# Where the first scores of layer one stand, and which weight sum GpSimd takes next

## The chip, the cores and the metric

The kernel runs on one core of a Trainium2 chip. The metric is the device time of one execution in microseconds (us); three runs of the kernel before took 2652.22, 2652.43 and 2653.41 us, median 2652.43. Lines such as L733 are lines of the kernel before. The engines are TensorE (PE, with its weight loads as PEld), VectorE (DVE), ScalarE (ACT), GpSimd (POOL) and SyncE (SP), which issues most transfers.

## The reference, cut to what matters

The inputs are `x` of 128 graphs × 64 nodes × 768 features in float32, an adjacency matrix for each graph, and for each of two layers three 768 × 768 weight matrices (left, right, linear), a bias and the scale and offset of a LayerNorm.

```python
h = jnp.maximum(_layernorm(x), 0.0)
for l in range(2):
    m_left, m_right = h @ W_left[l].T, h @ W_right[l].T
    u_left, u_right = h @ m_left^T / temper, h @ m_right^T / temper   # by graph, 64 x 64
    u = u_left * triu(adj, 1) + u_left * diag(adj) + u_right * triu(adj, 1)^T
    d = exp(u) * adj
    attention = d / (sum(d, axis=2) + 1e-10)
    h = relu(layer_norm(attention @ (h @ W_lin[l].T + b_lin[l]), ln_a[l], ln_b[l]))
out = x + h
```

The "scores" of this document are `u_left` and `u_right`; the tensors `m` are `m_left` and `m_right`.

## The kernel before

A part is 256 tokens (four graphs), kept with features on the partitions; there are 32 parts. Each layer has a first pass (scores and softmax, whose attention goes to DRAM) and a second pass (linear layer, attention product and LayerNorm). The change lies in the first pass of layer one (`l == 0` in the code), which is `pass_one`.

**Plain block and products.** The first pass computes `m_left` and `m_right`. For the first two parts it does so plainly: twelve chains of three 256 × 256 weight blocks (18 raw blocks, in `W[0, "raw"]`), each chain ending in a PSUM bank (C, D, X, Y in turn) that ACT copies into `m0` (first part) or `m1` (second part) at L889. The later parts go three at a time ("supers") by a fast scheme: 40 products (`PRODUCTS`) of a sum of weight blocks and a sum of token blocks; each product is four matmuls at L702, and its bank is read into several pieces of `m` with signs (`READS`; ACT at L910, DVE at L914 and L245). A super of three parts has 40 products; the third part of a super goes to `m2`. In layer one super 1 comes directly behind the plain block.

**Weight sums.** The fast scheme needs about a hundred sums of weight blocks (`W_OPS`). In layer one they are made while PE works on the plain block, and left in the 51 SBUF buffers `g`. `turn_of(slot)` runs twice in each product and hands out work by a model of time, `now = slot * 0.86`: as long as DVE's modelled clock is not ahead of `now`, `Weights.some` issues one more sum on DVE (0.62 us on its clock); if POOL's clock is not ahead, one on POOL (1.35 us). `some` walks the list of open sums in order and takes the first whose operands exist in the program's order; POOL may take only sums without a multiplier, among the first 40 open ones. POOL then goes on to the token sums (`Tokens.step`). Where a sum is the last use of an operand, it overwrites that operand's buffer (`emit`); other buffers come from `free`, which token sums use too.

**Staging.** During the plain block DVE does not read both operands of a sum from SBUF: `weights.stage` is a ring of PSUM banks (Z, V and the bank pair of the scores, sc), ACT first copies one operand into the next bank of the ring (L517), and DVE adds from there (L245, L522). The ring is set at L888 and cleared behind the plain block. 66 sums are staged. ACT's queue holds these copies, the copies into `m` (L889) and LayerNorm work of the next tokens (L412), in the order in which the code issues them; every engine runs its own queue in order.

**Scores and softmax.** `scores(k)` (L733) multiplies the tokens of super k by `m0`, `m1`, `m2` in small matmuls (32 × 95 columns) into sc. It loops over token halves and, inside, over six feature chunks. Each pair of chunks comes from one copy of L889, so a matmul waits only for the copies that its chunk needs. It is issued behind the fourth product of the next super (`i == SCORED`, SCORED is 3), and the banks of the first four products are read only then, since those reads overwrite `m`. `softmax(k)` is a chain of eight steps, put on slots three apart, starting ten slots behind the start of the next super: POOL masks (L745), DVE multiplies sc (L755), ACT takes Exp, DVE normalises, and eight transfers on SP store the attention.

Of the kernel before, what the change touches and what calls it, by code (L numbers as in the profile page):

```python
# [17 lines left out]
def kernel(  # L18
# [12 lines left out]
    nc = tc.nc  # L31
# [35 lines left out]
    def put(slot, *fs):  # L67
        plan.setdefault(slot, []).extend(fs)

    def put_all(slot, fs, step=1):  # L70
        for f in fs:
            if f is not None:
                put(slot, f)
            slot += step
        return slot
# [5 lines left out]
    def run(slot):  # L81
        if slot in plan:
            for f in plan.pop(slot):
                f()
        elif idle:
            f = idle.popleft()
            if f is not None:
                f()
        if background:
            background[0]()  # L90
# [84 lines left out]
    SCORED = 3  # L175
# [145 lines left out]
    KEEP = {}  # L321
# [155 lines left out]

    class Weights:
        def __init__(self, ops, plain, stay, extra=()):
            self.at, self.left, self.stay = {}, list(ops), stay  # L480
            self.uses = {}
            for _, a, _, b, _ in W_OPS:
                for v in (a, b):
                    self.uses[v] = self.uses.get(v, 0) + 1
            for v in range(18):
                self.uses[v] = self.uses.get(v, 0) + plain
            for f in FORMS:
                self.uses[f] = self.uses.get(f, 0) + 1
            self.stage = []
            self.mine = {id(t) for t in extra}  # L490
            self.extra = deque(extra)
# [36 lines left out]
            self.left.remove(op)  # L528
            return True

        def some(self, eng, reach=10):
            for op in self.left[:reach]:
                if op[1] in self.at and op[3] in self.at and (eng is nc.vector or op[2] == 1):
                    if eng is nc.vector and op[2] == 1 and any(o[2] != 1 and o[1] in self.at and o[3] in self.at
                                                               for o in self.left[:reach // 2]):
                        continue
                    return self.emit(eng, op)
            return False

        def need(self, v):  # L540
# [114 lines left out]
    def pass_one(l, start, final):  # L655
        with tc.tile_pool(name=f"one{l}", bufs=2, reuse_waits="tile") as sp, \
# [58 lines left out]
            def into(o, thirds=False):  # L715
                v, k, i = o // 6, o // 3 % 2, o % 3
                if thirds:
                    r, n = THIRDS[v]
                    return both[:, i * K2:(i + 1) * K2, :, k, r + n:r + WIDE]
                return M[v][:, i * K2:(i + 1) * K2, :, k, :]  # L720

            def scores(k):
                nq = 2 * len(SUPER[k])
                p = KEEP["scores"].rearrange("p a (q m) -> p (a q) m", m=P)
                for q in range(nq):
                    ht, m = HT[1, l, SUPER[k][q // 2]], M[q // 2]
                    for c in range(C):
                        for h in range(PAIR):
                            b = q % 2 * PAIR + h
                            mb = both[:, c, q // 2 * PB + b] if l and k == 0 else m[:, c, b]  # L730
                            mb = mb.rearrange("p k j -> p (k j)")
                            for e in (0, 32):
                                nc.tensor.matmul(p[h * S + e:h * S + e + 32, q, e:e + 95],  # L733
                                                 ht[:, c, b * S + e:b * S + e + 32], mb[:, e:e + 95],
                                                 start=(c == 0), stop=(c == C - 1))
# [45 lines left out]
            def softmax(k):  # L781
                CHAIN[k] = chain(k)
                return [lambda: next(CHAIN[k], None)] * 8

            mid = None
            if l == 0:
# [18 lines left out]
                def mid():  # L805
                    for f in turns[1:]:
                        f()
                    load_rows(0, 1, sp)
                    load_rows(0, 2, other)
                    for t in range(2):  # L810
                        nc.sync.dma_start(KEPT[0][t], HT[1, 0, t])
                    load_adj(0)
                    cols.extend([column("a_col", ln_a[0]), column("b_col", ln_b[0])])
# [8 lines left out]
            def bank_of(n):  # L822
                n %= BANKS
                return KEEP["CD"][n] if n < 2 else KEEP["XYZV"[n - 2]]

            weights, tokens = Weights(() if l else W_OPS, 2, True), TOKENS[l]
# [3 lines left out]
            clock = {"pool": 0.0, "vector": 0.0}  # L830

            def turn_of(slot):
                now = slot * 0.86 if l == 0 or slot >= 80 else slot * 0.6 + 20.8
                clock["vector"] = max(clock["vector"], now - 1.0) + sum(getattr(f, "vector", 0.0) for f in plan.get(slot, ()))
                run(slot)
                if fetch and slot >= start["weights"] and slot % 3 and free:
                    fetch.popleft()()
                if weights.left and slot >= start["weights"]:
                    while clock["vector"] <= now and weights.some(nc.vector):
                        clock["vector"] += 0.62  # L840
                    if clock["pool"] <= now and start["pool"] <= slot < start["tokens"]:
                        if weights.some(nc.gpsimd, 40):
                            clock["pool"] = max(clock["pool"], now) + 1.35
                if clock["pool"] <= now + 1.5 and tokens.step(slot):
                    clock["pool"] = max(clock["pool"], now) + 1.35
# [32 lines left out]
            slot = 0  # L878
            for n, (w, t) in enumerate(order):
                bank = bank_of(n % CHAINS)  # L880
                for j in range(3):
                    tok = HT[1, l, t][:, j * K2:(j + 1) * K2, :]
                    product(bank, weights.at[3 * w + j], [tok], j == 0, slot)
                    weights.used(3 * w + j)
                    if j == 2:
                        if n == 0 and mid:
                            mid()
                            weights.stage = [KEEP["Z"], KEEP["V"], KEEP["scores"][:, 0]]  # L888
                        nc.scalar.copy(into(6 * t + w), out_of(bank))  # L889
                    turn_of(slot + 1)  # L890
                    slot += 2
            weights.stage = []

            last = len(SUPER) - 1
            for k in range(FIRST_OF[l], len(SUPER)):
                assert slot == begins(k, l)
                if k:
                    put_all(slot + 2 * SCORED + 4, softmax(k - 1), 3)
                    put(slot + 2 * SCORED + 42, lambda k=k: load_adj(k, nc.scalar))
                if k == last:  # L900
                    final(slot, tokens)
                seen, waiting = set(), []

                def reads(i):
                    for o, c in READS[i]:
                        bank = out_of(bank_of(CHAINS * (k - 1) + i % CHAINS), k == 0, o)
                        to = into(o, k == 0)
                        if o not in seen:
                            seen.add(o)
                            nc.scalar.activation(to, bank, AF.Copy, scale=float(c))  # L910
                        elif abs(c) == 1:
                            added(nc.vector, to, "+" if c > 0 else "-", to, bank)
                        else:
                            nc.vector.scalar_tensor_tensor(to, bank, float(c), to, op0=ALU.mult, op1=ALU.add)  # L914

                for i, (f, t) in enumerate(PRODUCTS):
                    while l and f not in weights.at:
                        fetch.popleft()()
                    w, tok = weights.need(f), tokens.need(k, t)
                    product(bank_of(CHAINS * (k - 1) + i % CHAINS), w, tok, i < CHAINS, slot, TH if k else 2 * CUT)  # L920
                    tokens.used(k, t)
                    if k == last:
                        weights.used(f)
                    waiting.append(i)
                    if i == SCORED and k:
                        scores(k - 1)
                    if i >= SCORED or k == 0:
                        for n in waiting:
                            reads(n)
                        waiting = []  # L930
                    turn_of(slot + 1)
                    slot += 2
# [432 lines left out]
```

## Time and profile before

| what | value |
|---|---|
| runs | 2652.22, 2652.43, 2653.41 us; median 2652.43 |
| profiled execution, whole time | 2648.42 us |
| its span | 2646.6 us |
| mean granted clock of TensorE | 0.995 |
| busy, share of the span | PE 98%, PEld 84%, DVE 67%, POOL 67%, ACT 35% |
| transfers | 331.84 MB, mean 125 GB/s |

The span is the time from the first to the last instruction in the profile; the whole time has 1.8 us more around it. Shares are means over passes with different limits, so what an edit is worth is read in the stretch where it acts. A row of the time line has its start, its length, the engine, the line and operation, the tile written and the tiles read, the number of instructions merged and, in brackets, idle time ahead of it and what ended that. PE's records count double where one float32 matmul takes two instructions: a product of four matmuls is 8 records, the plain block's chain 24, the scores of two parts 192.

### The profile page before, as it was taken

To read this page: it belongs to the slowest core of one execution; us is meant where nothing else is said; L and a number is where in the kernel's file an instruction comes from. 1 tells how busy PE (TensorE), PEld (TensorE's weight loads), DVE (VectorE), ACT (ScalarE), POOL (GpSimd) and SP (SyncE) were. 2 spreads that over 40 slices of the span, in tenths; PEclk is the share of its full clock that TensorE was granted. 3 is DMA by queue.
4 is the path that set the end of the run, shared out by engine and by line. 5 is a ranking of instruction groups with operands and counts; after the bars stand their busy time and mean duration, and the time that the engine had idled before them with its cause. 6 is when DMAs were issued, how large, how long until landed. Compare 5 with 4: busy or idle time off the path is not lost. (4 is left out here: it accounts for less than half of the span.)

```text
span 2646.6 us, 47202 instructions
## 1 busy us (share of the span) xinstructions
PE 2591.6 (98%) x18122; PEld 2217.1 (84%) x18122; DVE 1780.6 (67%) x2888; ACT 935.4 (35%) x1969; POOL 1763.1 (67%) x1392
## 2 busy tenths in 40 slices
PE   9899999999999999999999999999999989999998
PEld 8788888888888888888798888888888878887886
DVE  7878787777768445554456667677666676666667
ACT  5522223223113244454542222122222335555453
POOL 4766676666668657676276666667666657878786
PEclk9999999999999999999999999999999999999999
DMA  7443534343421354445794424253532215555655
GB/s 220 113 111 86 124 93 110 93 119 79 98 60 56 123 156 149 159 139 182 219 282 101 121 68 108 71 129 93 136 98 70 67 49 157 157 167 166 177 161 146
DMA packets 258465, 331.84 MB, mean 125 GB/s; under 512 B 56002, under 2 KB 190402, under 8 KB 258242
## 3 DMA queue, kind: packets, MB, share of 16 engines
q1 hardware_dynamic: 241442, 320.56, 44.3%
q10 hardware_dynamic: 16800, 8.26, 1.2%
q8 instruction: 145, 2.38, 0.4%
q14 instruction: 78, 0.64, 0.1%
HBM read 213.39 MB, written 115.34 MB: 124 GB/s over the span
## 5 line engine op out<-in xcount | busy, mean ns | idle before, releaser
L245 POOL TENSOR_TENSOR g<-ht 128x512 f32<-128x512 f32 (+1 forms) x620 | 785.9, 1279 | 420.8 <-PE Z L702 71.6
L245 POOL TENSOR_TENSOR g<-g,g 128x512 f32<-128x512 f32 (+1 forms) x310 | 397.9, 1291 | 136.7 <-PE C L702 22.0
L245 POOL TENSOR_TENSOR g<-ht,g 128x512 f32<-128x512 f32 (+1 forms) x272 | 346.1, 1282 | 164.8 <-PE Z L702 42.8
L702 PE MATMUL X<-g,g 128*128 128x256 f32 (+1 forms) x1080 | 252.9, 377 | 6.0 <-DVE m L914 6.0
L1006 PE MATMUL Z<-g,g 128*128 128x256 f32 x1024 | 244.1, 380 | 3.5 <-ACT hl L300 3.2
L702 PE MATMUL C<-g,g 128*128 128x256 f32 x1008 | 239.7, 381 | 4.9 <-POOL g L245 2.2
L702 PEld LDWEIGHTS X<-g,g 128*128 128x128 f32 x1080 | 203.0, 191 | 34.8 <-DVE m L914 6.8
L702 PE MATMUL Y<-g,g 128*128 128x256 f32 (+1 forms) x968 | 225.7, 376 | 3.8 <-POOL g L245 3.8
L1006 PEld LDWEIGHTS Z<-g,g 128*128 128x128 f32 x1024 | 191.6, 190 | 35.8 <-issue 4.1
L379 ACT ACTIVATE ht<-ht,b_col,a_col 128x256 f32<-128x256 f32 x384 | 196.1, 591 | 69.0 <-DMA ht<-h 53.8
L702 PEld LDWEIGHTS C<-g,g 128*128 128x128 f32 x1008 | 190.5, 190 | 32.9 <-POOL g L245 3.5
L702 PE MATMUL Z<-g,g 128*128 128x256 f32 (+1 forms) x936 | 217.0, 375 | 0.0
L702 PE MATMUL D<-g,g 128*128 128x256 f32 x880 | 209.8, 381 | 1.8 <-POOL g L245 1.8
L702 PEld LDWEIGHTS Y<-g,g 128*128 128x128 f32 x968 | 182.0, 190 | 27.8 <-POOL g L245 4.2
L702 PE MATMUL V<-g,g 128*128 128x256 f32 (+1 forms) x840 | 194.6, 375 | 3.1 <-POOL g L245 1.6
L702 PEld LDWEIGHTS Z<-g,g 128*128 128x128 f32 x936 | 174.5, 190 | 23.1
L702 PEld LDWEIGHTS D<-g,g 128*128 128x128 f32 x880 | 168.1, 191 | 25.7 <-POOL g L245 2.5
L1006 PE MATMUL X<-g,g 128*128 128x256 f32 x768 | 182.7, 379 | 0.0
L702 PEld LDWEIGHTS V<-g,g 128*128 128x128 f32 x840 | 157.6, 191 | 23.3 <-POOL g L245 1.7
L1206 POOL TENSOR_TENSOR z<-z,b 128x768 f32<-128x768 f32 x62 | 112.7, 1829 | 81.7 <-DVE z L1203 77.2
L245 DVE TENSOR_TENSOR m<-m,Y 128x512 f32<-128x512 f32 (+2 forms) x196 | 126.5, 667 | 58.4 <-ACT m L910 35.7
L245 DVE TENSOR_TENSOR m<-m,D 128x512 f32<-128x512 f32 x180 | 118.2, 677 | 70.0 <-ACT m L910 51.3
(222 smaller groups left out, 4612.0 us busy)
## 6 DMA issues: line engine op xcount, KB each, us to landing
ht<-h SPq DMA_DIRECT2D x126, 768.0 KB, 6.3
h<-xb SPq DMA_DIRECT2D x124, 384.0 KB, 6.6
z<-z SPq DMA_DIRECT2D x128, 192.0 KB, 3.1
x<-z SPq DMA_DIRECT2D x128, 192.0 KB, 5.4
xr<-in_x_dram SPq DMA_DIRECT2D x120, 192.0 KB, 3.8
out_dram<-xr SPq DMA_DIRECT2D x120, 192.0 KB, 2.7
x<-in_x_dram SPq DMA_DIRECT2D x112, 192.0 KB, 5.4
g<-form SPq DMA_DIRECT2D x40, 256.0 KB, 5.6
```

The source lines that it names most:

```text
L245: (eng.tensor_add if sign == "+" else eng.tensor_sub)(o, a, b)
L379: nc.scalar.activation(ht, ht, AF.Relu, bias=cols[1][:, c:c + 1], scale=cols[0][:, c:c + 1])
L702: nc.tensor.matmul(o, w[:, c, g * P:(g + 1) * P], t, start=(new and g == c == at == 0), stop=(c == K2 - 1), skip_group_check=True)
L1006: nc.tensor.matmul(p[:, n], b[t][:, c, r * P:(r + 1) * P], w[s][:, c, :], start=(i in FIRST and i not in PRELOAD and n == c == 0), stop=(c ...
L1206: nc.gpsimd.tensor_add(zs[k], zs[k], rows["b"])
```

## The change

Three things are edited.

1. In layer one, `scores(0)` is issued directly behind the plain block instead of behind super 1's fourth product. The banks of super 1's first four products are then read one by one as each product is issued, and the softmax steps of the plain block start two slots behind the start of super 1 instead of ten.
2. From the ninth chain of the plain block on (`n == 8`) the staging ring is Z and V alone, since sc is to receive the scores.
3. `Weights.some` notes for each sum a modelled time at which it is made: `now + 6.0` on DVE, `now + 1.35` on POOL. For POOL the candidates are sorted by the later of their operands' times, all that lie before `now` counting alike, and the first is taken.

```diff
             self.at, self.left, self.stay = {}, list(ops), stay
+            self.made = {}
...
-        def some(self, eng, reach=10):
-            for op in self.left[:reach]:
+        def some(self, eng, reach=10, now=None):
+            ops = self.left[:reach]
+            if eng is nc.gpsimd:
+                ops = [op for op in ops if op[1] in self.at and op[3] in self.at and op[2] == 1]
+                ops.sort(key=lambda op: max(now, self.made.get(op[1], 0), self.made.get(op[3], 0)))
+            for op in ops:
...
-                    return self.emit(eng, op)
+                    if self.emit(eng, op):
+                        self.made[op[0]] = now + (6.0 if eng is nc.vector else 1.35)
+                        return True
+                    return False
...
                 bank = bank_of(n % CHAINS)
+                if n == 8:
+                    weights.stage = [KEEP["Z"], KEEP["V"]]
...
             weights.stage = []
 
+            if not l:
+                scores(0)
             last = len(SUPER) - 1
...
                 if k:
-                    put_all(slot + 2 * SCORED + 4, softmax(k - 1), 3)
+                    put_all(slot + (2 * SCORED + 4 if l or k > 1 else 2), softmax(k - 1), 3)
...
-                    if i == SCORED and k:
+                    if i == SCORED and l + k > 1:
                         scores(k - 1)
-                    if i >= SCORED or k == 0:
+                    if i >= SCORED or l + k < 2:
                         for n in waiting:
                             reads(n)
```

More of the change, by code (lines that the diff above doesn't have):

```diff
@@ L479, in __init__ @@
         def __init__(self, ops, plain, stay, extra=()):
-            self.at, self.left, self.stay = {}, list(ops), stay
+            self.at, self.left, self.stay, self.made = {}, list(ops), stay, {}
             self.uses = {}
@@ L838, in turn_of @@
                 if weights.left and slot >= start["weights"]:
-                    while clock["vector"] <= now and weights.some(nc.vector):
+                    while clock["vector"] <= now and weights.some(nc.vector, now=now):
                         clock["vector"] += 0.62
                     if clock["pool"] <= now and start["pool"] <= slot < start["tokens"]:
-                        if weights.some(nc.gpsimd, 40):
+                        if weights.some(nc.gpsimd, 40, now):
                             clock["pool"] = max(clock["pool"], now) + 1.35
```

## The prediction

> **What bounds the kernel now.** I read the page's totals first, then TensorE's waits, then the stretch in which its idle time lies, engine by engine.
>
> ```profile
> span 2646.6 us, 47202 instructions
> PE 2591.6 (98%) x18122; PEld 2217.1 (84%) x18122; DVE 1780.6 (67%) x2888; ACT 935.4 (35%) x1969; POOL 1763.1 (67%) x1392
> ```
>
> TensorE (PE) is busy for 98% of the span: all others work beside it, and only what makes it wait, or slows its clock, is on the path. Busy time in four stretches (columns: length, PE busy, granted clock, DMA share, GB/s):
>
> ```profile
> 0.00:74.89 74.89, 71.97 (x346) 1.00 0.80 215
> 74.89:99.49 24.60, 15.78 (x225) 0.79 0.50 127
> 99.49:200.00 100.51, 98.05 (x712) 1.00 0.39 100
> 200.00:2646.00 2446.00, 2405.85 (x16842) 1.00 0.45 124
> ```
>
> The edits act in layer one's first pass, around the end of the plain block. There, between 74.89 and 99.49 us, 8.8 of 24.6 us are idle and the clock averages 0.79. That is all there is to win or to double. PE's order of time there:
>
> ```profile
> 69.55 5.34 PE L702 MATMUL Y<-ht,g 128*128 128x256 f32 x24
> 77.08 2.51 PE L702 MATMUL C<-g,g 128*128 128x256 f32 x8 [2.19 <-POOL g L245]
> 81.39 3.78 PE L702 MATMUL D<-g,g 128*128 128x256 f32 x8 [1.79 <-POOL g L245]
> 84.96 2.03 PE L702 MATMUL X<-g,g 128*128 128x256 f32 x8
> 90.80 2.57 PE L702 MATMUL Y<-g,g 128*128 128x256 f32 x8 [3.80 <-POOL g L245]
> 93.30 5.16 PE L733 MATMUL sc<-m,ht 128*32 128x95 f32 x192
> 99.49 1.97 PE L702 MATMUL C<-g,g 128*128 128x256 f32 x8 [1.04 <-ACT m L910]
> ```
>
> The first row is the plain block's last product. Then come four products of the next stage with a wait ahead of three of them, then the scores of the plain block, then the fifth product. The fifth product's start, 99.49, is the mark I move: behind it PE is nearly gapless.
>
> **Scores ahead of four products.** The scores (L733) read the plain block's results, which ScalarE (ACT) copies into m (L889). PE finished the block at 74.89, but ACT's queue holds those copies behind the copies that it makes for VectorE's (DVE's) weight sums (L517):
>
> ```profile
> 76.96 0.58 ACT L889 COPY m<-D 128x512 f32<-128x512 f32 x1
> ...
> 81.97 0.58 ACT L889 COPY m<-X 128x512 f32<-128x512 f32 x1
> ...
> 83.04 0.59 ACT L517 COPY Z<-g 128x512 f32<-128x512 f32 x1
> 83.64 0.59 ACT L517 COPY V<-g 128x512 f32<-128x512 f32 x1
> ...
> 87.94 0.58 ACT L889 COPY m<-Y 128x512 f32<-128x512 f32 x1
> 88.42 0.59 ACT L517 COPY sc<-g 128x512 f32<-128x512 f32 x1
> ```
>
> The last one, m<-Y, runs 13 us after PE was done with Y. The order of the changed program keeps the same number of copies, 66, and the same place of m<-Y among them (one staged copy behind it). So scores that are issued at 74.89 cannot run at 74.89. Of 192 records, the chunks that need the last feature pair of the first token half wait for m<-X, those of the second half for m<-Y: 32 records can run at once, 96 after m<-X, and 64 (8 + 24 matmuls of the program, each twice in the trace) only after m<-Y. The four products, which today run in the gaps from 77 to 93, stand behind them. That is the step that I think decides: the filler for the wait has moved behind the wait.
>
> **Two staging banks instead of three.** From the ninth chain on, sc may no longer be a staging bank. Rows of VectorE today (start, length):
>
> ```profile
> 81.52 0.69 DVE L522 SCALAR_TENSOR_TENSOR g<-sc,g 128x512 f32<-128x512 f32 x1
> 82.32 0.69 DVE L522 SCALAR_TENSOR_TENSOR g<-Z,g 128x512 f32<-128x512 f32 x1
> 82.92 0.68 DVE L522 SCALAR_TENSOR_TENSOR g<-V,g 128x512 f32<-128x512 f32 x1
> ...
> 89.10 0.68 DVE L245 TENSOR_TENSOR g<-sc,g 128x512 f32<-128x512 f32 x1
> ```
>
> A sum takes 0.60 us from start to start (82.32 to 82.92), or about 0.80 where it reads the sum just before it (81.52 to 82.32). ACT is a bank ahead, so its 0.59 is hidden. With two banks a bank goes round DVE 0.68, ACT 0.59 and two hand-overs. The hand-over is small: the copy of 83.04 starts 0.03 behind the end of the sum of 82.32. So two sums need at least 0.68 + 0.59 + 2 × 0.035 = 1.34 where they take 1.20 today: 0.07 a sum. About 30 staged sums are left (DVE's order, the one after the switch to the one of 89.10), some nine of them at the slow pace, which hides the loss; 21 × 0.07 = 1.5 us. Three copies into m ahead of m<-Y also stand between two staged copies: ACT's pitch is 0.52 (87.42 to 87.94), so each sets the next staged copy to 2 × 0.52 behind the one before instead of 0.67, 0.37 later: 1.1 us. Sum 2.6 us at m<-Y. Ends: 0, if DVE's slower pairs and ACT's spare time hide it all, and 3.5, if none of the slow pairs hides any (30 × 0.07 = 2.1, plus 4 × 0.37). I take 2.6, since the row that today waits for a bank with three banks (the 83.04 copy, 0.03 behind its releaser) is already tight.
>
> **The clock.** Rows of four stretches, PE busy as the first and PEclk as the seventh column:
>
> ```profile
> 78.30:85.50 7.20, 5.41 (x14) 3.86 (x13) 6.89 (x12) 7.08 (x14) 4.95 (x4) 0.53 1.04 233
> 87.00:90.70 3.70, 0.00 (x0) 0.00 (x0) 3.70 (x6) 1.81 (x4) 2.49 (x3) 1.00 0.07 18
> 92.00:95.40 3.40, 3.40 (x60) 2.66 (x62) 3.33 (x9) 0.00 (x0) 2.64 (x3) 0.51 0.01 2
> 95.60:98.40 2.80, 2.80 (x140) 2.64 (x132) 0.46 (x2) 0.14 (x1) 2.80 (x4) 1.00 0.03 6
> ```
>
> After an idle stretch PE runs at half speed: for 3.4 us (92.0 to 95.4) after the 3.8 us wait, which costs 1.7 us, and from 78.3 on after one of only 2.19. In the changed kernel PE is idle from about 75 to m<-X, runs 96 records, and is idle again until m<-Y. I charge the last stretch one such slow time, 1.7 us; ends 0 and 3.4. The Trainium skill, "TensorE: Matmul & The Clock Gate", Part 1, says that the clock halves after an idle window of about 3.4 us and comes back after as much sustained work. The trace agrees on the way back (3.4 us), but the halving behind a 2.19 us gap is sooner than that sentence; by that section the 96 records would warm PE up, the idle time behind them, under 3.4 us, would not cool it, the 1.7 would be 0, and the sum below +0.5.
>
> **GpSimd's choice.** The sum is picked by when its operands were made, by a model time. GpSimd (POOL) takes 26 weight sums as before, DVE as many as before: only which, and in what buffers, changes. Its waits today:
>
> ```profile
> 58.41 5.11 POOL L245 TENSOR_TENSOR g<-g,g 128x512 f32<-128x512 f32 x4 [3.98 <-DVE g L522]
> 69.47 6.33 POOL L245 TENSOR_TENSOR g<-g,g 128x512 f32<-128x512 f32 x5 [5.95 <-ACT Z L517]
> 88.13 2.61 POOL L245 TENSOR_TENSOR g<-ht,g 128x512 f32<-128x512 f32 x2 [2.53 <-DVE g L522]
> 97.26 1.43 POOL L745 TENSOR_TENSOR wm<-adj,tri 128x256 f32<-128x256 f32 x2
> ```
>
> The long one at 63.5 to 69.47 is for a staged copy that must have read a buffer before POOL overwrites it; the changed order has the same wait at the same copy. POOL being on time earlier helps only if DVE then waits less, and DVE's long waits before the block's end are for ACT:
>
> ```profile
> 40.30 0.69 DVE L522 SCALAR_TENSOR_TENSOR g<-sc,g 128x512 f32<-128x512 f32 x1 [2.98 <-ACT sc L517]
> 57.04 0.69 DVE L522 SCALAR_TENSOR_TENSOR g<-sc,g 128x512 f32<-128x512 f32 x1 [2.56 <-ACT sc L517]
> ```
>
> These staged copies stand behind LayerNorm work in ACT's queue, which the change leaves. I take 0; ends −1.3 and +1.3, one POOL sum (6.33 / 5) earlier or later in front of a staged copy.
>
> **Softmax eight slots earlier.** POOL's two mask products (1.43 us) now run ahead of a token sum of the fourth product. That sum ended at 88.13 + 2.61 = 90.74, where the fourth product started (90.80); now at 90.74 + 2.6 (it waits for DVE's weight sums) + 1.43 = 94.8. The product will start at 98 or later: 3 us of cover, so nothing. The chain's four products on DVE fall into time in which DVE idles today (4.27 us before 100.37):
>
> ```profile
> 100.37 0.69 DVE L245 TENSOR_TENSOR m<-m,D 128x512 f32<-128x512 f32 x1 [4.27 <-ACT m L910]
> ```
>
> On SyncE's queue the eight attention stores move ahead of four stores of h and eight loads of x, for supers whose turn is tens of us off; on ACT's the Exp and its table move forward, with idle time around them. All 0; if this cover is gone, the price is a wait at the next product, at most the 1.43.
>
> **Sum.** m<-Y starts at 87.94 + 2.6 = 90.5 and ends at 91.1. Meanwhile m<-X ends at 82.55 + some 2 = 84.6; the 96 records take half of 5.16 us, 2.6, or 5.2 at half clock, and end by 89.8: hidden. Then 64 of 192 records, 1.72 us: 92.9 (with 0.04 of hand-over). Then four products at 1.78 (a third of the 24 records that took 5.34 at 69.55), 7.1: 100.0. With 1.7 for the clock the fifth product starts at 101.7, 2.2 later than 99.49. What the early reads save (the 1.04 wait for ACT ahead of the fifth product) is in this, since the products' results are read as they come. Nothing later gives it back or takes more. The profiled execution took 2648.42 us and would take 2650.6; it stands 4.0 under the median of the runs, 2652.43, so the forecast is 2654.6. What a measurement of this kernel can tell from no change is about 0.2%, 5.3 us.
>
> **The rivals.**
> - *Two banks cost nothing* (the change of banks does nothing that can be seen): m<-Y ends at 88.5, the fifth product starts at 88.5 + 1.76 + 7.1 + 1.7 = 99.1, and the time is −0.4, 2652.0. For it: DVE's 0.80 pairs. Against: 21 sums at 0.60.
> - *Clock at full for the last stretch*: the 96 records bring the clock back as 92.0 to 95.4 did, and the gap behind them is too short to lose it: +0.5, 2652.9. Against: the 2.19 us gap that was enough. It is what the Trainium skill's section on the clock gate, named above, would give.
> - *DVE gets through its sums sooner* (the other side): POOL's better choice removes stalls of DVE, and the whole queue, m<-Y with it, is early. Each us there is a us here, until the products' own waits end it. It decides where m<-Y starts 2.2 us earlier than I have it (88.3); at 83.0 the kernel is faster by 0.2%; at 82 the time is 2652.43 − 6.3 = 2646.1. For it: POOL's 3.98 and 5.95 of waiting. Against: DVE's waits are ACT's.
> - *A longer queue*: with two banks every copy waits for a sum and every sum for a copy, and all 30 go at the pace of the 0.80 rows: 30 × 0.2 = 6.0 instead of 2.6, +5.6, 2658.0.
> - *Half clock through the whole stretch*: 1.72 + 7.1 at half speed adds 8.8 instead of 1.7: +9.3, 2661.7. For it: 7 us at 0.53 from 78.3. Against: there PE had gaps, and 3.4 us without one brought it back.
>
> **How the numbers follow.** The forecast holds 0.50, the neutral banks 0.15, the full clock 0.15, the sooner DVE 0.07, the longer queue 0.08, the long half clock 0.05. The first three lie within 0.2%: same 0.80; faster 0.07; slower 0.13. The forecast's own bounds are lag 0 to 3.5 and clock 0 to 3.4: from 97.4 (−2.1) to 104.3 (+4.8), 2650.3 to 2657.2. With POOL's 1.3 below and part of the slow rivals above I put 2649 to 2659.
>
> **What would show it.** Right: scores of the plain block in three pieces, the last one right behind m<-Y, with PE idle for over 8 us ahead of m<-X; m<-Y at 90 to 91.5; the fifth product at 100 to 103; DVE's staged sums at about 0.67 apart. Wrong: m<-Y before 87, the scores in one piece at 75, PE gaps among the four products, or a time that moved with no move of the fifth product.

## The result, and the profile after

The changed kernel takes 2656.03 us (median of 20 runs, 2653.46 to 2661.99), the kernel before, run beside it, 2651.60 us (20 runs, 2648.43 to 2653.43). The ratio is 1.0020, with a 95% interval of 1.0014 to 1.0026, so 3.7 to 6.9 us slower. The time lies inside the predicted range, 1.4 us above the forecast of 2654.6. Whether it is over the 0.2% that was set as the bound of "no change" can't be told: the bound lies in the interval. The profiled execution took 2653.46 us.

The totals of the changed kernel's page: the work is the same, and TensorE (PE) is as busy as before.

```profile
span 2651.7 us, 47194 instructions
PE 2590.2 (98%) x18122; PEld 2217.7 (84%) x18122; DVE 1784.6 (67%) x2888; ACT 935.5 (35%) x1969; POOL 1762.7 (66%) x1392
```

PE's time line around the end of the plain block, after the change (start, length, line and operation, count, idle time ahead and what ended it):

```profile
74.98 0.86 PE L740 MATMUL sc<-m,ht 128*32 128x95 f32 x32
86.03 3.69 PE L740 MATMUL sc<-m,ht 128*32 128x95 f32 x96 [10.18 <-ACT m L898]
92.47 2.66 PE L740 MATMUL sc<-m,ht 128*32 128x95 f32 x64 [2.76 <-ACT m L898]
95.06 2.47 PE L709 MATMUL C<-g,g 128*128 128x256 f32 x8
...
100.82 1.89 PE L709 MATMUL Y<-g,g 128*128 128x256 f32 x8
102.54 1.89 PE L709 MATMUL C<-g,g 128*128 128x256 f32 x8
```

The scores run in three pieces of 32, 96 and 64 records. PE is idle for 10.18 us ahead of the second and 2.76 us ahead of the third, both times for a copy that ScalarE (ACT) makes, and the four products stand behind all of it. The fifth product starts at 102.54 instead of 99.49. The two copies that were waited for, in ACT's time line of the changed kernel:

```profile
85.40 0.58 ACT L898 COPY m<-X 128x512 f32<-128x512 f32 x1
...
91.84 0.58 ACT L898 COPY m<-Y 128x512 f32<-128x512 f32 x1
```

The copy m<-Y came 3.90 us later than before (87.94). VectorE (DVE) shows the ring of two banks ahead of it:

```profile
81.41 0.69 DVE L522 SCALAR_TENSOR_TENSOR g<-Z,g 128x512 f32<-128x512 f32 x1
82.01 0.68 DVE L245 TENSOR_TENSOR g<-V,g 128x512 f32<-128x512 f32 x1
82.75 0.69 DVE L522 SCALAR_TENSOR_TENSOR g<-Z,g 128x512 f32<-128x512 f32 x1
83.36 0.68 DVE L245 TENSOR_TENSOR g<-V,g 128x512 f32<-128x512 f32 x1
...
92.94 0.69 DVE L245 TENSOR_TENSOR g<-Z,g 128x512 f32<-128x512 f32 x1 [0.31 <-ACT Z L517]
```

Two sums take 1.34 us (81.41 to 82.75), and the last staged sum starts at 92.94 where it started at 89.10.

Behind the fifth product the prediction had nothing more. Yet the scores of super 1 started at 168.73 us before and at 175.27 after: 72.73 us behind the fifth product instead of 69.24. PE's waits between 99 and 176 us, after the change (line that waited, what it waited for, total, times, longest):

```profile
PE X L709 <- DVE m L925: 1.0, 1, 1.0
PE Y L709 <- DVE m L245: 0.9, 1, 0.9
PE C L709 <- DVE m L245: 0.6, 1, 0.6
```

All are products that wait until DVE has read a bank. Before, no product between the fifth and super 1's scores waited for DVE. What held DVE up can be seen in its time line: at the first wait the softmax, at the others a load.

```profile
118.06 0.53 DVE L774 TENSOR_SCALAR s<-s 128x4 f32<-128x4 f32 x1
118.63 0.18 DVE L775 RECIPROCAL s<-s 128x4 f32<-128x4 f32 x1
118.84 1.35 DVE L776 TENSOR_TENSOR adj<-adj,s 128x256 f32<-128x256 f32 x1
120.12 0.68 DVE L925 SCALAR_TENSOR_TENSOR m<-X,m 128x512 f32<-128x512 f32 x1
...
142.15 1.02 DVE L336 BATCH_NORM_STATS2 st<-x 128x6 f32<-128x384 f32 x2 [2.98 <-DMA x<-in_x_dram]
```

The read of bank X at 120.12 stands behind 2.06 us of softmax steps (118.06 to 120.12); the product into X starts at 120.94, as soon as that read is over. At 142.15 DVE has waited 2.98 us for x. Before, the same steps took 0.72 us (118.19 to 118.91), and DVE's first step on x had no wait:

```profile
118.19 0.13 DVE L767 TENSOR_SCALAR s<-s 128x4 f32<-128x4 f32 x1
...
118.57 0.43 DVE L769 TENSOR_TENSOR adj<-adj,s 128x256 f32<-128x256 f32 x1
118.91 0.68 DVE L914 SCALAR_TENSOR_TENSOR m<-X,m 128x512 f32<-128x512 f32 x1
...
134.91 1.01 DVE L336 BATCH_NORM_STATS2 st<-x 128x6 f32<-128x384 f32 x2
```

The queue of SyncE tells why x is late, in the changed kernel:

```profile
122.49 5.09 SPq L785 DMA_DIRECT2D att<-wm  x8
127.68 5.15 SPq L461 DMA_DIRECT2D h<-xb  x4
132.94 6.83 SPq L361 DMA_DIRECT2D x<-in_x_dram  x8
```

and in the kernel before:

```profile
118.30 5.16 SPq L461 DMA_DIRECT2D h<-xb  x4
123.63 9.47 SPq L361 DMA_DIRECT2D x<-in_x_dram  x8
133.22 5.73 SPq L778 DMA_DIRECT2D att<-wm  x8
```

The eight attention stores hold the queue for 5.09 us and now stand ahead of the loads of x, which are issued 9.3 us later: 3.05 us of that is the later fifth product, and 6.3 comes behind it. The stores and DVE's softmax steps are the part of the change that the prediction put at nothing.

### The profile page after: what moved, and what is told of

Its sections match the earlier page's. It is cut to its first block, busy times and chain, and to the rows that moved or that the text cites. A ratio compares the mean times of both kernels' runs of the same rounds, so it can differ in the third digit from the quotient of the medians.

```text
span 2651.7 us, 47194 instructions
## 1 busy us (share of the span) xinstructions
PE 2590.2 (98%) x18122; PEld 2217.7 (84%) x18122; DVE 1784.6 (67%) x2888; ACT 935.5 (35%) x1969; POOL 1762.7 (66%) x1392
## 5 line engine op out<-in xcount | busy, mean ns | idle before, releaser
L740 PE MATMUL sc<-m,ht 128*32 128x95 f32 x6144 | 142.0, 249 | 26.0 <-ACT m L898 12.9
```

The lines of the kernel that those rows point to most:

```text
L740: nc.tensor.matmul(p[h * S + e:h * S + e + 32, q, e:e + 95], ht[:, c, b * S + e:b * S + e + 32], mb[:, e:e + 95], start=(c == 0), stop=(c ...
```

## The experiments

Two marks are read in every trace: the start of the fifth product, and the start of super 1's scores 40 products later. Between them lies the softmax. One profile stands for each kernel, and behind the second mark single profiles stray by several us (the kernel with the choice alone is 1.10 behind the kernel before at super 1's scores, and 2.97 behind it, 250.65 against 247.68, at super 2's); whole times therefore go by the intervals, and the marks only say where in the first 176 us the time arises. The ratios are to the kernel before, run beside each on the same chip (for the change the 20 runs given above; for the experiments 33 runs, median 2652.33 us for the first four of the table, 2653.56 us for the other four).

| kernel | m<-Y | fifth product | super 1's scores | difference | ratio, 95% interval |
|---|---|---|---|---|---|
| before | 87.94 | 99.49 | 168.73 | 69.24 | 1 |
| after | 91.84 | 102.54 | 175.27 | 72.73 | 1.0020 (1.0014 to 1.0026) |
| without the choice | 90.89 | 101.44 | 174.28 | 72.84 | 1.0013 (1.0004 to 1.0022) |
| choice alone | 89.03 | 100.59 | 169.83 | 69.24 | 1.0003 (0.9994 to 1.0012) |
| softmax ten slots behind | 91.75 | 100.84 | 170.34 | 69.50 | 1.0002 (0.9993 to 1.0011) |
| two banks alone | 90.55 | 101.91 | 171.15 | 69.24 | 1.0016 (1.0008 to 1.0025) |
| stores late | 90.97 | 100.06 | 171.07 | 71.01 | 1.0014 (1.0005 to 1.0023) |
| clock kept | 91.19 | 100.33 | 175.11 | 74.78 | 1.0006 (0.9997 to 1.0015) |
| scores moved, nothing else early | 90.63 | 101.35 | 170.51 | 69.16 | 1.0003 (0.9993 to 1.0012) |
| copies ahead | 78.11 | 92.32 | 172.68 | 80.36 | 1.0005 (0.9995 to 1.0015) |

The theory after the result: two banks and the choice make m<-Y late, the clock adds some, and the early softmax adds waits behind the fifth product. The rival: the softmax costs nothing, and what is lost behind the fifth product is only the lateness of the work ahead of it.

**Without the choice.** The changed kernel, with GpSimd (POOL) taking the first sum that is ready, as before.

```diff
-            if eng is nc.gpsimd:
+            if False:
```

> The changed kernel, with GpSimd again taking the first possible sum in the list; scores, two banks and softmax stay as changed. Theory: the new choice starts GpSimd at 16.2 us beside VectorE's first unstaged sums, which took 4.05 us for three instead of 1.90, and so all of VectorE's queue is about 1 us late; without it the first staged sum is at about 20.3 instead of 21.46, the last copy into m at about 90.8 instead of 91.84, and the kernel about 1 us faster than the changed one. Rival (the late start is the transfers' or chance): the last copy stays at 91.5 to 92, and the time that of the changed kernel.

m<-Y came at 90.89 instead of 91.84, and the fifth product at 101.44 instead of 102.54: the choice costs about 0.8 us here at m<-Y, since 0.16 of the 0.95 is the landing of the weights (DVE's row of three sums, shown below, starts at 15.91 here and at 16.07 after the change). The difference stayed at 72.84, so the loss behind the fifth product is not the choice's. The whole time, 2655.50 us, can't be told from that of the full change.

**The choice alone.** The kernel before, with `made` and the sorted candidates of the change, three banks, and the scores and softmax where they were.

```diff
+            if eng is nc.gpsimd:
+                ops = [op for op in ops if op[1] in self.at and op[3] in self.at and op[2] == 1]
+                ops.sort(key=lambda op: max(now, self.made.get(op[1], 0), self.made.get(op[3], 0)))
```

> The kernel before with GpSimd's choice alone. Theory: VectorE's queue is about 1 us late by the same contention; the fourth product waits for a token sum that waits for VectorE's sums, so the fifth product starts at about 100.5 instead of 99.49: +1 us on the kernel before. Rival (the choice is neutral): 99.5 and no difference. Other rival (the choice helps when the scores stay where they were): the fifth product before 98.5 and the kernel 1 us faster.

The marks moved by 1.10 each. The place is the start of the kernel, where DVE sums operands that are both in SBUF. Rows of DVE and then of POOL, before:

```profile
15.64 1.90 DVE L522 SCALAR_TENSOR_TENSOR g<-g,g 128x512 f32<-128x512 f32 x3 [0.66 <-DMA g<-in_w_right_dram]
...
18.38 1.73 DVE L245 TENSOR_TENSOR g<-g,g 128x512 f32<-128x512 f32 x1 [0.24 <-DMA g<-in_w_right_dram]
...
18.30 2.95 POOL L245 TENSOR_TENSOR g<-g,g 128x512 f32<-128x512 f32 x2 [16.57 <-DVE g L245]
```

and in the changed kernel:

```profile
16.07 4.05 DVE L522 SCALAR_TENSOR_TENSOR g<-g,g 128x512 f32<-128x512 f32 x3 [0.65 <-DMA g<-in_w_right_dram]
...
16.15 3.42 POOL L245 TENSOR_TENSOR g<-g,g 128x512 f32<-128x512 f32 x2 [14.43 <-DMA g<-in_w_right_dram]
```

With the choice alone the row is the same as in the changed kernel:

```profile
16.09 4.05 DVE L522 SCALAR_TENSOR_TENSOR g<-g,g 128x512 f32<-128x512 f32 x3 [0.66 <-DMA g<-in_w_right_dram]
```

POOL now starts its two sums beside DVE's three instead of behind them, and each of DVE's takes 1.35 us instead of 0.63. All five kernels with the choice show 4.04 to 4.06 us for these three sums, the other five 1.89 or 1.90. In the kernel before it is a later sum of DVE (18.38) that runs beside POOL, and it takes 1.73 us. Counted from the start of those three, the first staged sum comes at 5.39 us in both kernels with the choice that are shown (21.46 − 16.07 after the change, 21.48 − 16.09 with the choice alone) and at 4.61 before (20.25 − 15.64): 0.78 later. The landing of the weights, 0.45 later in this execution, comes on top. Counted from it, both marks moved by 0.65, and only that much of the 1.10 is the choice's. The Trainium skill, "SBUF — State Buffer", section "SBUF: two separate sides", says that a VectorE instruction with two SBUF inputs and a GpSimd instruction that reads SBUF exclude one another for the length of the whole instruction. The rows come near that: three times 0.63 and two POOL sums of 1.27 in turn make 4.43 as an estimate, against 4.05 measured, so some 0.4 us must have overlapped. DVE's staged sums, with one operand in PSUM, stayed at 0.68.

**Softmax ten slots behind.** The changed kernel, with the softmax of the plain block where it was.

```diff
-                    put_all(slot + (2 * SCORED + 4 if l or k > 1 else 2), softmax(k - 1), 3)
+                    put_all(slot + 2 * SCORED + 4, softmax(k - 1), 3)
```

> The changed kernel with the softmax of the plain block again ten slots behind the start of super 1. Theory: the fifth product stays at about 102.5, but the eight loads of x are issued at about 127 instead of 132.9, VectorE does not wait 3 us for them at 139 to 142, the three waits of PE for VectorE between 118 and 155 (0.97, 0.92 and 0.65) go, and scores(1) start at about 172 instead of 175.3: 3 us faster than the changed kernel, about 1.5 over the kernel before. Rival (VectorE is simply 3 us late and meets PE anyway): the waits stay in some form, scores(1) at about 175, and the time within 0.5 us of the changed kernel.

The difference fell from 72.73 to 69.50, PE shows no wait for DVE between the marks, and the ratio is 1.0002, its interval wholly below that of the full change. So at the marks the early softmax is the largest part of the loss, 3.23 of 6.54 us; between the two kernels without the choice, softmax early and not, it is 72.84 against 69.16. Its x loads were issued ahead of the stores again:

```profile
125.67 9.29 SPq L361 DMA_DIRECT2D x<-in_x_dram  x8
```

The fifth product was also 1.70 sooner than after the full change, which was not expected, although m<-Y was only 0.09 sooner. That is the clock. Windows of PE (columns: stretch, length, PE busy, granted clock, DMA share, GB/s), the changed kernel first:

```profile
86.00:89.70 3.70, 3.67 (x96) 0.56 0.52 117
89.70:92.40 2.70, 0.01 (x4) 1.00 0.00 0
92.60:95.90 3.30, 3.30 (x66) 0.51 0.00 0
```

and the kernel with the softmax ten slots behind:

```profile
92.60:95.90 3.30, 3.30 (x74) 1.00 0.00 0
```

The same scores in the same stretch ran at half clock in one kernel and at full clock in the other.

**Two banks alone.** The kernel before, with the short ring and nothing else of the change.

```diff
+                if n == 8:
+                    weights.stage = [KEEP["Z"], KEEP["V"]]
```

> The kernel before with the staging ring cut to two banks from the ninth chain on, nothing else. Theory: VectorE's last staged sum moves from 89.10 to about 91.8, staged sums are 0.67 to 0.74 apart where they were 0.60; the token sum of the fourth product waits for them, so that product starts at about 93.5 instead of 90.80 and the fifth at about 102 instead of 99.49: +2.5 us on the kernel before. Rival (the ring costs nothing where scores do not wait): the last sum moves, but the kernel stays within 0.5 us.

ACT's copy and the fifth product in this kernel, where the scores still stand behind the fourth product:

```profile
90.55 0.58 ACT L891 COPY m<-Y 128x512 f32<-128x512 f32 x1
```

```profile
101.91 1.96 PE L702 MATMUL C<-g,g 128*128 128x256 f32 x8 [1.04 <-POOL g L245]
```

m<-Y moved by 2.61 us (90.55 − 87.94) and the fifth product by 2.42, with the order of before. The ratio, 1.0016, has an interval above 1. So the ring alone makes the kernel slower.

**Scores moved, nothing else early.** The changed kernel without the choice and with the softmax where it was: the ring of two and the moved scores are left.

```diff
-            if eng is nc.gpsimd:
+            if False:
...
-                    put_all(slot + (2 * SCORED + 4 if l or k > 1 else 2), softmax(k - 1), 3)
+                    put_all(slot + 2 * SCORED + 4, softmax(k - 1), 3)
```

> The changed kernel without GpSimd's choice and without the early softmax: scores behind the plain block, and two banks. Theory from the runs so far: scores(1) started at 168.7 in the kernel before, 171.15 with two banks alone, 170.3 with two banks, the scores moved and GpSimd's choice, which alone costs 1.1; so moving the scores by itself gives 1.9 back, and here scores(1) start at about 169.2, the kernel +0.5 us on the one before. Rival (the gain of e3_softmax_ten_slots was a lucky phase of the clock): 171 or later, +2 us or more.

Against two banks alone the marks are 0.56 and 0.64 sooner (101.35 and 170.51): the move itself gains a little, even with the filler behind the wait; the four products run here without the gaps that they had. It would have gained more but for the clock:

```profile
91.26 1.81 PE L740 MATMUL sc<-m,ht 128*32 128x95 f32 x64 [2.41 <-ACT m L898]
93.00 3.34 PE L709 MATMUL C<-g,g 128*128 128x256 f32 x8
```

The product C took 3.34 us; at full clock one takes 1.89 (the product at 102.54 after the change). The 170.51 lies between the 169.2 that I expected and the rival's 171. From m<-Y to the fifth product it took 10.72 us here and 9.09 with the softmax ten slots behind (`e3_softmax_ten_slots` in the text above), so the gain there was in part a favourable phase of the clock, as the rival says. With the difference of 1.63 taken off, super 1's scores would start at 168.9 here, as an estimate.

**Stores late.** The changed kernel, whose last softmax step, with the eight attention stores, goes where it went before; the DVE steps stay early.

```diff
-                    put_all(slot + (2 * SCORED + 4 if l or k > 1 else 2), softmax(k - 1), 3)
+                    steps = softmax(k - 1)
+                    put_all(slot + (2 * SCORED + 4 if l or k > 1 else 2), steps[:-1], 3)
+                    put(slot + 2 * SCORED + 25, steps[-1])
```

> The changed kernel, with the softmax of the plain block early as changed but its last step (the transposes and the eight stores of the attention on SyncE's queue) back at its old slot. Theory (what the early softmax costs is mostly the stores standing ahead of the stores of h and the loads of x): the loads of x are issued at about 128 instead of 132.9, VectorE's wait of 3 us for them goes and with it PE's waits of 0.92 and 0.65 at 151 to 155; the wait of 0.97 at 120.94, for VectorE's softmax work, stays. From the fifth product to scores(1) it takes about 70.8 us (changed kernel 72.7, kernel before 69.2). Rival (VectorE's softmax steps do the harm, by coming among the reads): 72 us or more, though the loads are early.

The loads of x stand ahead of the stores again, and the wait of the first kind is left:

```profile
128.12 9.47 SPq L361 DMA_DIRECT2D x<-in_x_dram  x8
```

```profile
119.10 1.97 PE L709 MATMUL X<-g,g 128*128 128x256 f32 x8 [1.06 <-DVE m L927]
```

The difference fell to 71.01, near the 70.8 expected, and DVE's wait for x to 0.78. Of the 3.23 between 72.73 and 69.50 the place of the stores makes 1.72, the softmax steps in DVE's order 1.51. In the whole time this is not seen: 2655.84 us and 1.0014, with an interval that overlaps those of the full change and of the softmax ten slots behind.

**Clock kept.** The changed kernel with 88 and 36 added transposes on PE ahead of the chunks that wait for m<-X and m<-Y, into a part of the scores' bank that nobody reads. They add work that only keeps PE busy through the gaps.

```diff
+                        if l == k == 0 and c == C - K2 and q in (0, 2):
+                            for _ in range({0: 88, 2: 36}[q]):
+                                nc.tensor.transpose(KEEP["scores"][:, 1, :P], KEEP["ident"], KEEP["ident"])
```

> The changed kernel with work that nobody reads on PE in its two gaps: 88 transposes of the identity into the free bank of the scores ahead of the matmuls that wait for m<-X, 36 ahead of those that wait for m<-Y (the result is the same, 124 small matmuls are added). Theory: PE's clock stays at full, the last 64 records of the scores take 1.7 instead of 2.66 us and the first product behind them 1.9 instead of 2.47; the fifth product starts at about 101.1 instead of 102.54, 1.4 us sooner, and the kernel is 1.4 us faster than the changed one. Rival (the long records are something else than the clock): no change.

With the gaps filled the last scores ran at full clock, and the fifth product came at 100.33, 2.21 sooner than after the change (m<-Y itself was 0.65 sooner here; from it to the fifth product it took 9.14 us instead of 10.70):

```profile
91.88 1.51 PE L743 MATMUL sc<-m,ht 128*32 128x95 f32 x64
```

But super 1's scores started at 175.11, only 0.16 sooner. DVE met the loads of x earlier and waited longer, 4.87 us instead of 2.98:

```profile
142.43 1.02 DVE L336 BATCH_NORM_STATS2 st<-x 128x6 f32<-128x384 f32 x2 [4.87 <-DMA x<-in_x_dram]
```

So the clock's loss is real at the fifth product and worth nothing at the second mark as long as the loads are late. The ratio, 1.0006, is lower than that of the full change by more than the second mark would give, though the intervals touch; what behind that mark would make it so, one profile can't tell.

**Copies ahead.** An attempt at a version better than both: the scores behind the block, three banks until the block's end, then two through super 1's start; no choice, softmax ten slots behind, and DVE's modelled clock set 10 us forward, so that fewer weight sums are planned ahead of ACT's copies into m.

```diff
+                if n == 6:
+                    clock["vector"] += 10.0
...
-            weights.stage = []
-
+            if not l:
+                weights.stage = [KEEP["Z"], KEEP["V"]]
+                scores(0)
...
+                if l or k > 1:
+                    weights.stage = []
```

> A version meant to beat both. Scores behind the plain block, softmax at its old slot, GpSimd as before, three banks to the end of the plain block; and fewer of VectorE's sums are issued ahead of the last copies into m: its modelled clock is set 10 us forward at the seventh chain, so ScalarE's queue is short when the block ends, and the sums that are left are issued, staged through Z and V, during super 1. Theory: m<-Y runs at about 76 to 77 instead of 91.84, the scores follow the block with a gap of 2 us at most, the clock stays up, the fifth product starts near 88.5; then the waits come back at products that need late weight and token sums, so that scores(1) start at about 167, 1.7 us sooner than before; with the clock kept, 2 to 3 us faster than the kernel before. Rival (VectorE's work and the buffers it frees set the time of super 1 whatever comes first): the gain at the fifth product is all given back, scores(1) at 168.7 or later, no gain.

Now the scores do run in one piece, and the fifth product starts 7.17 sooner than before, though not at the 88.5 expected: m<-Y is at 78.11, and the scores then wait until DVE has read the last sum that was staged in their own bank (to 79.54). None of it is left at the second mark. PE's time line of this kernel:

```profile
79.60 5.78 PE L740 MATMUL sc<-m,ht 128*32 128x95 f32 x192 [3.39 <-DVE g L245]
...
92.32 1.89 PE L709 MATMUL C<-g,g 128*128 128x256 f32 x8
...
101.22 1.99 PE L709 MATMUL Y<-g,g 128*128 128x256 f32 x8 [1.72 <-POOL g L245]
...
112.69 3.78 PE L709 MATMUL Y<-g,g 128*128 128x256 f32 x8 [4.28 <-POOL g L245]
```

The difference is 80.36. PE now waits three times for sums that POOL makes (the third, 1.58 us, is ahead of the product at 97.51). The wait has moved, not gone: in this kernel the sums set when super 1's products can run, though PE was ready for them sooner. That they come late because the weight sums ahead of them were put off is my reading and wasn't measured by itself. No version here beats the kernel before.

## Why the prediction was right, and where it was not

**Scores ahead of four products: right in its path, wrong in its weight.** Three pieces of 32, 96 and 64 records; idle time of 10.18 us ahead of m<-X, where over 8 was put; the last piece 0.05 behind the end of m<-Y (91.84 + 0.58 = 92.42, 92.47). So m<-Y does set when the fifth product starts. But the move, of which the prediction says "That is the step that I think decides", is not what costs: against two banks alone it made both marks sooner, by 0.56 and 0.64 us. The price came from the shorter ring that the move needs, from GpSimd's choice and from the softmax.

**Two staging banks: right, and its size too.** 1.34 us for two sums was worked out and 1.34 measured; 2.6 us at m<-Y was put and 2.61 measured with the banks alone. The changed kernel shows it too: its last staged sum ahead of the short ring is 1.17 us later than before (69.85 against 68.68) and the last of all 3.84, so 2.67 arose in between. The rival "two banks cost nothing" fell with that run, and so did "a longer queue": the sums that depend on one another did not spread their pace to the others.

**GpSimd's choice: wrong, "I take 0".** It costs 0.78 us ahead of the first staged sum, inside the 1.3 that stood as its end. The step looked at POOL's waits alone. What it left out is that a POOL sum which starts sooner runs beside DVE sums with both operands in SBUF and makes each of these twice as long. With it m<-Y was at 91.84, 0.34 beyond the 91.5 that was to show the step right; 0.43 us of its lateness is the landing of the weights (16.07 against 15.64), which no step had foreseen. The rival "DVE gets through its sums sooner" went the other way, by that cause.

**The clock: right in kind, 1.7 put, about 1.6 measured.** From m<-Y to the fifth product it is 10.70 us after the change and 9.09 with the softmax ten slots behind, where the stretch was at full clock: 1.61. It is not a fixed price: the rival "clock at full" came true in two of the kernels that keep the moved scores, and did not in three.

**The fifth product: 102.54,** in the 100 to 103 put down; 3.05 later than before instead of 2.2. m<-Y was 1.34 later than the 90.5 of the sum, by the choice and the landing, and the way from there took 10.70 us instead of 11.2.

**Softmax eight slots earlier: the step that failed.** "All 0; if this cover is gone, the price is a wait at the next product, at most the 1.43", and "Nothing later gives it back or takes more". POOL's two mask products were indeed hidden, but the price arose elsewhere. The softmax's DVE steps stand ahead of a bank's read (1.0 us of PE), and the stores ahead of the loads of x make DVE 2.98 us late (0.9 and 0.6 us of PE); with the restarts the difference between the marks grew by 3.23 to 3.49 us. "Supers whose turn is tens of us off" was read as slack. It was too little: the loads of x were issued 9.3 us later (6.3 of it behind the fifth product), and DVE was at their place in its order before they had landed.

**The sum.** Ring 2.42, choice 1.10 (0.45 of it the landing of the weights), softmax 3.23 and the move with its half clock −0.64 make 6.11 of the 6.54 us at the second mark (175.27 − 168.73); the prediction had 2.2 and stopped there. The profiled execution was 5.04 us slower (2653.46 − 2648.42), the ratio says 5.3 (0.0020 × 2652). So the forecast of the time, 1.4 below the median, was nearer than that of its parts, and that is partly luck: beside the changed kernel the kernel before took 2651.60 us instead of 2652.43, and the change measured, 4.4 us between the medians, is twice the 2.2 that was forecast. That the early softmax costs time in the whole rests on one pair of kernels (1.0020 against 1.0002, intervals 0.0003 apart). The pair without the choice points the same way, 1.0013 against 1.0003, but its intervals overlap; clock kept, which has the early softmax too, is at 1.0006. At the marks the cause is shown, in the whole time it is likely. How the rest of its 3 us, and of the 2.4 of the ring, spread to the end stays open, since the whole times and the second mark do not follow one another from kernel to kernel: two banks alone, +2.42 at the mark and 1.0016; clock kept, +6.38 and 1.0006.

## What to carry to other kernels

Work that is moved ahead can run only when the slowest in-order queue that feeds it gets there, so look for the last copy or sum that it reads. Ask also what the work put behind it had waited for: the four products cost nothing there, since the fourth of them had waited for a sum until 90.80 anyway, and the price was the bank that the ring gave up. When a step is moved, follow each of its instructions into each queue, DMA issues too, and ask what was next there: here eight small stores, 5.09 us of the queue, came ahead of the loads, which were issued 6.3 us later behind the fifth product. And a gain ahead of a fixed wait is no gain: two edits that brought the fifth product 2.2 and 7.2 us forward lost nearly all of it, or more, at the next waits.

## What the runs showed of the hardware

**Half clock depends on where the gap falls.** A gap of 2.41 us ahead of the last scores was followed by full clock in the kernel with the softmax ten slots behind (granted clock 1.00) and by half in the one with the scores moved and nothing else early, where the granted clock was 0.66 in the next 3.3 us:

```profile
91.30:94.60 3.30, 3.30 (x68) 0.66 0.00 0
```

The cost lies between 0 and 1.6 us for the same program text around it.

Narrow windows (0.2 us) of the traces show what decides. Between 70 and 110 us the granted clock changes only at points that lie whole multiples of 3.41 us apart: 78.42, 85.24, 92.07 and 95.48 in the kernel before, 78.98, 89.22, 92.64 and 96.05 after the change, 88.92, 92.34 and 95.75 with the scores moved and nothing else early, 80.47 and 90.71 with the softmax ten slots behind. What counts is how long PE is busy between two such points. It was busy for 1.08 us from 88.92 to 92.34, and the clock fell at 92.34, in the midst of work; it was busy for 1.74 us from 90.71 to 94.12, one step of 3.41 on, and the clock stayed up. In the ten traces, over the same 40 us, the busiest such stretch that the clock fell behind held 1.42 us of work (choice alone, 75.29 to 78.70), and the least busy one at full clock that it did not fall behind 1.62 (stores late, 89.82 to 93.23). So the gap's length alone does not tell; how it lies among these points does.

The Trainium skill, "TensorE: Matmul & The Clock Gate", Part 1, says that the window in which activity is judged runs freely and isn't tied to the kernel's start; that fits this. That it takes an idle window of about 3.4 us to halve the clock does not: gaps of 2.41 and 2.76 us were enough here.

**GpSimd lengthens VectorE's sums when both operands are in SBUF,** 0.63 to 1.35 us for 128 × 512 in float32, and not when one is in PSUM (0.69 us at 22.42 in the changed kernel, beside a POOL sum that starts at 22.23). The softmax steps show it too: `adj<-adj,s` took 1.35 us in the changed kernel, where a row of before has it at 0.4:

```profile
L769 DVE TENSOR_TENSOR adj<-adj,s 128x256 f32<-128x256 f32 x1 | 0.4, 426 | 0.0
```

A POOL sum ran beside the long one (118.65, for 1.26 us). That POOL is the cause in this second place was not tested.
